# Keeping step 1's exponentials in an attention kernel, and who issues its block swaps

## The chip, the cores and the metric

The kernel runs on one core of a Trainium2 chip. A time is the device time of one execution in microseconds; the median of the runs is compared. TensorE (PE) multiplies matrices into PSUM, VectorE (DVE), ScalarE (ACT) and GpSimd (POOL) work element by element, and SyncE (SP) issues DMAs. GpSimd issues some of the DMAs too.

## The reference

`x` is 8 × 512 × 512 (batch, sequence, model). Sixteen heads of 32 columns attend within each batch, a condition token is projected and added to queries and keys, and the result is added to x:

```
Q, K, V = heads(x @ Wq.T + bq), heads(x @ Wk.T + bk), heads(x @ Wv.T + bv)
cQ, cK  = Q + heads(cond @ Wq.T + bq), K + heads(cond @ Wk.T + bk)
attn    = softmax(cQ @ cK.T / sqrt(32))          # 512 x 512 for each head
out     = x + merge(attn @ V)
```

## The kernel before

The work is cut into 32 steps, t = 0 to 31. Step t is a batch b = t // 4 and a group of four heads, r = t mod 4, which fill the 128 partitions (32 columns each). In what follows "tile t" is what belongs to step t.

For each tile the scores are first computed with queries on the partitions (`row_scores`, L641), in four blocks of 128 queries (`qc`), four heads each, one PSUM bank for a head. VectorE takes the negated row maxima from them (`row_max`, with single reductions of one bank at L589, or a reduction over a pair of neighbouring banks at L650). ScalarE takes the exponentials with that maximum as bias and adds up their sums (`denominators`, L693). These exponentials have the queries on the partitions, and the product with V needs the keys there. There are two ways on:

- An ordinary tile throws them away, keeping the sums. Its maxima are split into three bfloat16 parts (`split_max`, on GpSimd, L707 to L710) and transposed by a DMA (`turn_max`, L719). The scores are computed a second time with the keys on the partitions: four bursts (`exponentials`), each a small matmul that brings the maxima in (L745) and four matmuls for the scores (L748), then ScalarE's exponentials (L758).
- A kept tile (`KEPT`, steps 2 to 28) writes the exponentials of its first two query blocks to a place in SBUF (`room`). VectorE transposes them in blocks of 32 × 32 (`turn_kept`, L660, four instructions of 128 × 1024). What is left is to exchange the blocks between partitions. `swap_kept` does it by DMA for the six pairs of partition groups, in three rounds (`move`) of six transfers of 128 KB, L674: round 0 copies one block of each pair aside, round 1 copies the other over it, round 2 copies the first from aside. A round's transfer waits for the landing of its pair's transfer before. Rounds 0 and 1 are issued at the end of the step before, round 2 within the step. Only the other two query blocks are computed a second time, in two bursts (`exponentials_of_rest`, L766, L777, L787).

In step t, TensorE does the second scores of tile t, the row scores of tile t + 1 (and the first block of t + 2), the product with V of tile t − 1 (`weighted`, L792 for ordinary, L808 for kept tiles: first the half that was computed again, then the kept half) and one part of the projections of the next batch. These are computed by Strassen's scheme (`product`, L461) from sums of blocks of x (`combine_x`, L387 to L391, four sums for each batch) and of W. The list `MADE` spreads them over steps of a batch, three to a step. A kept step has three parts (`thirds`), an ordinary one four. After the products, ScalarE copies and GpSimd adds (`first_by_others`, L535 to L537 for q and k, L1220 and L1221 for v), or VectorE adds with the bias (`other_products`, L551 and L486). `send` transposes the result on VectorE (L880), scales it and adds x on GpSimd (L881, L882), and stores it through SP (L885). SP also loads x for the next batch (L173) and for the residual (L191).

The order on PE, DVE, ACT and POOL is that of the program text; the order of SP's DMAs is planned by the framework. Each queue is worked in order, so an instruction that waits holds up those behind it. The functions `begin` and `released` choose the PSUM banks of a part by the order in which they came free.

Steps with t mod 4 = 0 make the sums of x for the next batch on GpSimd, in parts 2 and 3, just before the rounds 0 and 1 of the next tile (t mod 4 = 1) are issued. Before the main loop, step 0 makes the first half of the sums for batch 1 on VectorE (L387, L388 at the end of its third part) and step 1 the second half on GpSimd.

Of the kernel before, what the change touches and what calls it, by code (L numbers as in the profile page):

```python
# [17 lines left out]
def kernel(  # L18
# [38 lines left out]
    nc = tc.nc  # L57
    P = 128
# [9 lines left out]
    T = B * G  # L68
    HS = S // 2

    KEPT = range(2, T - 3)
    KQ = NS // 2

    const = ctx.enter_context(tc.tile_pool(name="const", bufs=1))
# [54 lines left out]
    def advance():  # L129
        turn[0] += 1  # L130
# [67 lines left out]
    def bias_residual(t):  # L198

        if turned_by_vector(t):  # L200
            bias = bvs[:, t % G, :].unsqueeze(1).broadcast_to([P, NB, BL])
        else:
            bias = bvl.broadcast_to([P, S])
        nc.gpsimd.tensor_tensor(xr[t], xr[t], bias, ALU.add)  # L204
# [3 lines left out]

    def room(t):

        at = (t - KEPT[0]) % 3 * 4
        return store[:, at : at + 4].rearrange("p g c (h s) -> p g c h s", s=P)

    ring_at = [0]

    places = [*range(4, 16), *range(8, 12)]

    def chunk():

# [321 lines left out]
    def other_products(n, b, u, dens, small, at, bias=False):  # L541

        dens()
        one_, two_ = banks(at[0]), banks(at[1])
        product(n, b, u, 4, one_[:, :HS])
        product(n, b, u, 5, one_[:, HS:])
        small()
        product(n, b, u, 2, two_[:, :HS], (1,))
        product(n, b, u, 3, two_[:, HS:])
        c1, c12, c2, c22 = parts_of(n, b, u)  # L550
        nc.vector.tensor_tensor(c12, one_[:, HS:], c12, ALU.add)  # L551
        if bias and n != "v":
            plus(n, b, u, 1, c2, halves(one_), twice(c22))
        else:
            nc.vector.tensor_tensor(c2, halves(one_), twice(c22), ALU.add)
        plus(n, b, u, 0, c1, halves(two_), c1)
        if n != "v":
            for g in range(2):
                qkT[n, b * G + u * 2 + g] = pair_of(b * G + u * 2, n)[:, g, :]
# [104 lines left out]

    def swap_kept(t, move, last=nc.gpsimd):

        def part(a, g):
            return kept[t][a * BL : (a + 1) * BL, g].rearrange("p c h s -> p (c h s)")

        for n, (a, g) in enumerate(APART):  # L670
            at = (n + 2) % HG * BL
            aside = between[at : at + BL, n // HG].rearrange("p i s -> p (i s)")
            to, of = [(aside, part(a, g)), (part(a, g), part(g, a)), (part(g, a), aside)][move]
            (last if move == 2 or move == 0 and n >= 3 else nc.sync).dma_start(to, of)  # L674

    def denominators(t, qc, w=HG, js=range(HG)):

# [387 lines left out]
    row_max(1, 2)  # L1065
    denominators(1, 2)
    other_products("v", 0, 0, nothing, nothing, (0, 2))
    advance()
    exponentials(0, 2)
    row_max(1, 3)  # L1070
    split_max(1)
    turn_max(1)
    first_products("v", 0, 1, lambda: denominators(1, 3), nothing, 1)
    combine_x(1, 0)
    advance()
    exponentials(0, 3)
    row_max(2, 0)
    other_products("v", 0, 1, lambda: denominators(2, 0), nothing, (0, 2))

    MADE = [  # L1080
        (n, u, product)
# [26 lines left out]
        else:  # L1108
            released(1, 2, 4, 5, 6, 7, 0, 3)

    def bursts(s, i):

        if s not in KEPT:
            return [(s, i)]
        return [(s, i - 2)] if i >= 2 else []

    TURNED = {(0, 2): 2, (1, 2): 1, (2, 2): 1}
    TURNED_FIRST = {(0, 2): 1, (1, 2): 1, (2, 2): 1, (3, 2): 1}
    turned = {}

    def turn_more(t, i, after):

        behind = t - 1 not in KEPT
        for _ in range((TURNED if t in KEPT else TURNED_FIRST).get((i, after), 0)):
            if t + 1 in KEPT:
                n = turned[t + 1] = turned.get(t + 1, -1) + 1
                turn_kept(t + 1, n)
        if (t, i, after) == (1, 1, 1) or t in KEPT and (i, after) == (0, 2):
            turn_x((t - 1) % G + ((t - 1) // G + 2) * NC)

    def thirds(t, made):

        b, r = divmod(t, G)
        of = (t - 1) // G + 1
        begin(0, HG)
        turn_more(t, 0, 0)
        row_max_aside(t + 1, 1)
        max_aside(t + 1, 1)
        row_max(t + 1, 2, False, HG)
        turn_more(t, 0, 1)  # L1140
        denominators(t + 1, 1, None, (1, 2, 3, 0))
        denominators(t + 1, 2, HG)
        weighted(t - 1, banks(0), banks(1), nothing)
        turn_more(t, 0, 2)
        load_blocks()
        one_item(of, *next(made), (2, 3), ignore, nothing)
        released(0, 1, 4, 5, 6, 7, 2, 3)
        for i in (1, 2):
            begin(HG)
            exponentials_of_rest(t, i - 1)  # L1150
            turn_more(t, i, 0)
            rows = (t + 1, 3) if i == 1 else (t + 2, 0)
            row_max(*rows, False, HG)
            turn_more(t, i, 1)
            if i == 1:
                if t + 1 in KEPT:
                    swap_kept(t, 2)
                split_max(t + 1)
                if t + 1 in KEPT:
                    turn_max(t + 1)  # L1160
                else:
                    swap_kept(t, 2)
            dens = lambda js=range(HG): denominators(*rows, HG, js)
            n, u, kind = next(made)
            if kind == "first":
                products(of, n, u, kind, False, dens, nothing, None)
                turn_more(t, i, 2)
            elif n == "v":
                small = nothing
                if t + 1 not in KEPT:  # L1170
                    small = lambda: transpose_max(t + 1, banks(2), nc.scalar.copy)
                other_shared(of, n, u, dens, (0, 3), small, lambda: turn_more(t, i, 2))
                released(1, 2, 4, 5, 6, 7, 0, 3)
            else:
                products(of, n, u, kind, False, dens, nothing, False)
                turn_more(t, i, 2)
            if i == 1:
                aparts[t] = masked(t)
            load_blocks()
            if i == 2:  # L1180
                if r == 0:
                    combine_x(b + 1, 1, nc.gpsimd)
                load_residual(t + 1)
                if t + 1 in KEPT:
                    for move in range(2):
                        swap_kept(t + 1, move)
            else:
                bias_residual(t)
                if r == 0:
                    combine_x(b + 1, 0, nc.gpsimd)  # L1190

# [42 lines left out]
        else:  # L1234
            other_products(n, b, u, dens, nothing, at, True)

    for t in range(1, T - 3):
        b, r = divmod(t, G)
        made = iter(MADE[(t - 1) % G * 3 :])
        if t in KEPT:  # L1240
            thirds(t, made)
            continue
        items = "PVPP" if t - 1 in KEPT else "VPPP"
        for i, item in enumerate(items):
            rows = (t + 1, i + 1) if i < 3 else (t + 2, 0)
            scores = bursts(t, i)
            alone = not scores
            w = 0 if alone else HG
            begin(w)
            for u, kc in scores:  # L1250
                if u in KEPT:
                    exponentials_of_rest(u, kc)
                else:
                    exponentials(u, kc)
            turn_more(t, i, 0)
            row_max(*rows, False, w)
            turn_more(t, i, 1)
            if i == 2:
                split_max(t + 1)
                turn_max(t + 1)  # L1260
            dens = lambda js=range(HG): denominators(*rows, w, js)

            def last():
                if i == 0 and r == 1:
                    combine_x(b + 1, 1, nc.gpsimd)
                if i == 1 and r == 0:
                    combine_x(b + 1, 0, nc.gpsimd)

            if item == "P":
                products((t - 1) // G + 1, *next(made), alone, dens, last, None if (t, i) == (1, 3) else True)  # L1270
            else:
                dens()
                last()
                if alone:
                    weighted(t - 1, banks(4), banks(5), nothing)
                    released(6, 7, 0, 1, 2, 3, 5, 4)
                else:
                    weighted(t - 1, banks(0), banks(1), nothing)
                    released(2, 3, 1, 4, 5, 6, 7, 0)
            turn_more(t, i, 2)  # L1280
            if i == 2:
                aparts[t] = masked(t)
                if t > 1:
                    bias_residual(t)
            load_blocks()
            if i == 3:
                load_residual(t + 1)
            if i == 3:
                for move in range(2):
                    swap_kept(t + 1, move)  # L1290
    row_of[0] = None
    places[:] = 6, 7, 16, 17, 12, 13, 14, 15, 8, 9, 10, 11
    ring_at[0] = 0
# [218 lines left out]
```

## Time and profile before

| | us |
|---|---|
| median of 3 runs (666.71 to 668.23) | 666.72 |
| the profiled execution | 667.76 |
| its span | 666.0 |
| PE busy | 652.7 |
| DVE busy | 589.9 |
| ACT busy | 542.0 |
| POOL busy | 423.6 |

The profile is one execution with every instruction's start and duration. "Busy" is the time in which an engine worked on something; the span is the time from the first instruction to the end of the last, and the execution's time has a little more around it. A wait row names who waited, for whom, the total, how often and the longest. A timeline row gives start, duration, engine, line, operation, what is written and read, how many instructions are merged, and in brackets how long the engine was idle ahead of it and what ended that.

### The profile page before, as it was taken

What the parts mean: (1) busy time and instruction counts of PE and PEld (TensorE: products, weight loads), DVE (VectorE), ACT (ScalarE), POOL (GpSimd) and SP (SyncE); (2) the same over time, 40 slices, a digit from 0 to 9 for tenths busy, and PEclk for the clock granted to TensorE, in tenths of its full rate; (3) what the DMA queues carried; (4) which work ended last, traced back from release to release, by engine and by line L of the source; (5) the groups of instructions that cost most, each with busy time, mean ns of one, the idle gap of its engine ahead of it and who ended that gap; (6) DMA issues with size and microseconds to landing.
All of it is one profiled execution on the core that took longest, in us unless ns stands there. A gap on an engine that the chain in (4) does not pass through costs nothing.

```text
span 666.0 us, 24768 instructions
## 1 busy us (share of the span) xinstructions
PE 652.7 (98%) x9812; PEld 349.4 (52%) x9812; DVE 589.9 (89%) x821; ACT 542.0 (81%) x1378; POOL 423.6 (64%) x668
## 2 busy tenths in 40 slices
PE   9999999999999999999999999999999999999993
PEld 7345445555555555555555555555555555555421
DVE  3698899999999999998999999999999989995793
ACT  2479988889888888988888898888889888887771
POOL 3541345787666876659757696667875597576531
PEclk9999999999999999999999999999999999999998
DMA  6633157778777787877897787779877757786111
GB/s 178 105 51 63 31 122 161 163 165 187 173 152 174 161 190 154 189 156 167 171 190 167 169 191 172 160 150 170 196 165 176 169 133 175 149 181 138 18 18 32
DMA packets 246183, 97.14 MB, mean 146 GB/s; under 512 B 228842, under 2 KB 229354, under 8 KB 246068
## 3 DMA queue, kind: packets, MB, share of 16 engines
q1 hardware_dynamic: 232644, 62.65, 49.3%
q0 software_dynamic: 11664, 31.87, 17.3%
q8 instruction: 77, 1.26, 0.9%
q10 hardware_dynamic: 1760, 1.05, 0.5%
q14 instruction: 38, 0.31, 0.1%
HBM read 19.75 MB, written 8.39 MB: 42 GB/s over the span
## 4 chain that ended last, share of the span: by engine, by line
PE 95%; DMA 2%; SPq 1%; DVE 1%; issue 0%; DVEq 0%
PE psum L461 43%; PE psum L641 19%; PE psum L808 15%; PE psum L777 7%; PE psum L792 3%; PE psum L766 3%; PE psum L748 2%; SPq L270 1%; PE psum L404 1%; DMA w_q<-in_L_cond_Wq_dram 1%; PE psum L745 1%; PE psum L1336 1%; PE psum L818 1%; DMA store<-in_x_dram 1%; DMA w_k<-in_L_cond_Wk_dram 0%; PE psum L843 0%
## 5 line engine op out<-in xcount | busy, mean ns | idle before, releaser
L693 ACT ACTIVATE psum<-psum,nmax 128x512 f32<-128x512 f32 x263 | 174.8, 670 | 5.0 <-DVE nmax L589 3.9
L589 DVE TENSOR_REDUCE nmax<-psum 128x1 f32<-128x512 f32 x219 | 140.5, 678 | 22.2 <-PE psum L641 19.6
L693 ACT ACTIVATE store<-psum,nmax 128x512 f32<-128x512 f32 x190 | 130.3, 700 | 33.3 <-DVE nmax L589 23.8
L650 DVE TENSOR_REDUCE nmax<-psum 128x2 f32<-128x1024 f32 x127 | 153.7, 1211 | 1.3 <-PE psum L641 1.3
L674 POOL DMA_DIRECT2D store<-store x243 | 121.7, 504 | 48.1 <-DMA store<-store 36.2
L641 PE MATMUL psum<-kT,qT 32*128 32x512 f32 x1024 | 146.7, 616 | 0.0
L787 ACT ACTIVATE store<-psum 128x512 f32<-128x512 f32 x216 | 111.5, 603 | 22.6 <-PE psum L777 22.6
L660 DVE STREAM_TRANSPOSE store<-store 128x1024 f32<-128x1024 f32 x108 | 129.5, 1217 | 0.0
L808 PE MATMUL psum<-store,v 128*32 128x256 f32 x1728 | 99.3, 381 | 0.0
L808 PEld LDWEIGHTS psum<-store,v 128*32 128x32 f32 x1728 | 53.2, 110 | 54.1 <-ACT wT_q L628 19.7
L641 PEld LDWEIGHTS psum<-kT,qT 32*128 32x128 f32 x1024 | 57.8, 183 | 37.3 <-issue 20.2
L881 POOL TENSOR_TENSOR res<-res,recs 128x512 f32<-128x512 f32 x30 | 31.4, 1047 | 69.0 <-DVE res L880 68.9
L693 ACT ACTIVATION_READ_ACCUMULATOR psum<-psum,nmax 128x1 f32 x263 | 56.3, 214 | 0.0
L777 PE MATMUL psum<-qT,kT 32*128 32x256 f32 x864 | 55.8, 373 | 0.0
L461 PE MATMUL psum<-wc_v,xc 128*32 128x256 f32 x768 | 47.7, 379 | 0.0
L204 POOL TENSOR_TENSOR xr<-xr,bvs 128x512 f32<-128x512 f32 x30 | 38.4, 1279 | 12.2 <-DMA x<-in_x_dram 11.4
L461 PE MATMUL psum<-xc,wc_k 128*32 128x256 f32 x720 | 44.5, 379 | 0.0
L461 PE MATMUL psum<-xc,wc_q 128*32 128x256 f32 x720 | 44.5, 379 | 0.0
L777 PEld LDWEIGHTS psum<-qT,kT 32*128 32x128 f32 x864 | 42.3, 184 | 3.4
L693 ACT ACTIVATION_READ_ACCUMULATOR store<-psum,nmax 128x1 f32 x190 | 40.8, 215 | 0.0
L882 POOL TENSOR_TENSOR res<-res,xr 128x512 f32<-128x512 f32 x30 | 38.4, 1279 | 2.4
L758 ACT ACTIVATE store<-psum 128x512 f32<-128x512 f32 x56 | 28.9, 603 | 9.3 <-PE psum L748 7.2
(198 smaller groups left out, 1046.3 us busy)
## 6 DMA issues: line engine op xcount, KB each, us to landing
store<-store SPq DMA_DIRECT2D x243, 128.0 KB, 2.8
store<-store POOLq DMA_DIRECT2D x243, 128.0 KB, 3.7
out_dram<-res SPq DMA_DIRECT2D x122, 64.0 KB, 3.6
xr<-in_x_dram SPq DMA_DIRECT2D x120, 64.0 KB, 3.4
x<-in_x_dram SPq DMA_DIRECT2D x112, 64.0 KB, 3.0
w_q<-in_L_cond_Wq_dram SPq DMA_DIRECT2D x4, 256.0 KB, 5.3
w_v<-in_L_cond_Wv_dram SPq DMA_DIRECT2D x16, 64.0 KB, 2.5
w_k<-in_L_cond_Wk_dram SPq DMA_DIRECT2D x16, 48.0 KB, 3.0
```

The lines of the kernel that those rows point to most:

```text
L204: nc.gpsimd.tensor_tensor(xr[t], xr[t], bias, ALU.add)
L461: nc.tensor.matmul(pt[r], still[:, r], moving, start=(kc == kcs[0]), stop=(kc == kcs[-1]))
L589: nc.vector.tensor_reduce(nmax[t][:, qc, j : j + 1, 0], pt, AX.X, ALU.max, negate=True)
L641: nc.tensor.matmul(pt, qkT["q", t][r, qc * P : (qc + 1) * P], qkT["k", t][r, :], start=True, stop=True,)
L650: nc.vector.tensor_reduce(nmax[t][:, qc, pr * 2 : pr * 2 + 2, 0], pt, AX.X, ALU.max, negate=True)
L660: nc.vector.transpose(e, e)
L674: (last if move == 2 or move == 0 and n >= 3 else nc.sync).dma_start(to, of)
L693: nc.scalar.activation(to, of, AF.Exp, bias=nmax[t][:, qc, j, :], accum_out=sums[t][:, qc, j, :],)
L777: nc.tensor.matmul(bank[j][:, i * HS : (i + 1) * HS], qkT["k", t][r, kc * P : (kc + 1) * P], qkT["q", t][r, rest], start=False, stop=(i == 1),
L787: nc.scalar.activation(e[:, i, :], bank[pr * 2 + i], AF.Exp)
L808: nc.tensor.matmul(pt[j * HD : (j + 1) * HD, half * HS : (half + 1) * HS], vs[b % 2][:, kc, (g * HG + j) * HD : (g * HG + j + 1) * HD], e, ...
L882: nc.gpsimd.tensor_tensor(y, y, xr.pop(t), ALU.add)
```

## The change

Step 1 becomes a kept step, so `KEPT` begins at 1 and the separate form of an ordinary step in the main loop goes. Its tile gets the place in SBUF that the rule of three places gives it, and the ring of places for the exponentials of step 0 changes so that they don't overlap. Its four transpositions and rounds 0 and 1 of its swaps are in step 0, and round 2 is in step 1 as in any kept step. Step 0's last row maxima of tile 1 are taken in four single reductions instead of two and a pair. All four sums of x for batch 1 are made by GpSimd in step 0. Finally, round 0 of every tile is shared out differently: before, SP issued three of its six transfers and GpSimd three. Now SP issues all six for tiles with t mod 4 = 1, and one of six for the others. Round 1 stays with SP, round 2 with GpSimd.

```
-    KEPT = range(2, T - 3)
+    KEPT = range(1, T - 3)
...
-        at = (t - KEPT[0]) % 3 * 4
+        at = (t + 1) % 3 * 4
...
-    places = [*range(4, 16), *range(8, 12)]
+    places = [*range(4, 8), *range(12, 16)]
...
     def swap_kept(t, move, last=nc.gpsimd):
+        later = 6 if t % 4 == 1 else 1
...
-            (last if move == 2 or move == 0 and n >= 3 else nc.sync).dma_start(to, of)
+            (last if move == 2 or move == 0 and n >= later else nc.sync).dma_start(to, of)
...
     other_products("v", 0, 0, nothing, nothing, (0, 2))
+    turn_kept(1, 0)
     advance()
     exponentials(0, 2)
-    row_max(1, 3)
+    row_max(1, 3, True)()
     split_max(1)
     turn_max(1)
     first_products("v", 0, 1, lambda: denominators(1, 3), nothing, 1)
-    combine_x(1, 0)
+    turn_kept(1, 1)
+    turn_kept(1, 2)
+    combine_x(1, 0, nc.gpsimd)
     advance()
     exponentials(0, 3)
     row_max(2, 0)
     other_products("v", 0, 1, lambda: denominators(2, 0), nothing, (0, 2))
+    turn_kept(1, 3)
+    combine_x(1, 1, nc.gpsimd)
+    aparts[0] = masked(0)
+    for move in range(2):
+        swap_kept(1, move)
...
-        for _ in range((TURNED if t in KEPT else TURNED_FIRST).get((i, after), 0)):
+        for _ in range(TURNED.get((i, after), 0)):
...
-        if (t, i, after) == (1, 1, 1) or t in KEPT and (i, after) == (0, 2):
+        if (i, after) == (0, 2):
             turn_x((t - 1) % G + ((t - 1) // G + 2) * NC)
...
-                bias_residual(t)
+                if t > 1:
+                    bias_residual(t)
...
-    for t in range(1, T - 3):
-        b, r = divmod(t, G)
-        made = iter(MADE[(t - 1) % G * 3 :])
-        if t in KEPT:
-            thirds(t, made)
-            continue
-        items = "PVPP" if t - 1 in KEPT else "VPPP"
-        for i, item in enumerate(items):
...
-                    swap_kept(t + 1, move)
+    for t in KEPT:
+        thirds(t, iter(MADE[(t - 1) % G * 3 :]))
```

More of the change, by code (lines that the diff above doesn't have):

```diff
@@ L1109, in products @@
             released(1, 2, 4, 5, 6, 7, 0, 3)
[L1111 to L1115, printed above, removed]
     TURNED = {(0, 2): 2, (1, 2): 1, (2, 2): 1}
-    TURNED_FIRST = {(0, 2): 1, (1, 2): 1, (2, 2): 1, (3, 2): 1}
     turned = {}
     def turn_more(t, i, after):
-        behind = t - 1 not in KEPT
-        for _ in range((TURNED if t in KEPT else TURNED_FIRST).get((i, after), 0)):
+        for _ in range(TURNED.get((i, after), 0)):
             if t + 1 in KEPT:
@@ L1235, in one_item @@
             other_products(n, b, u, dens, nothing, at, True)
-    for t in range(1, T - 3):
-        b, r = divmod(t, G)
-        made = iter(MADE[(t - 1) % G * 3 :])
-        if t in KEPT:
-            thirds(t, made)
-            continue
-        items = "PVPP" if t - 1 in KEPT else "VPPP"
-        for i, item in enumerate(items):
[L1245 to L1289, printed above, removed]
-                    swap_kept(t + 1, move)
+    for t in KEPT:
+        thirds(t, iter(MADE[(t - 1) % G * 3 :]))
     row_of[0] = None
```

## The prediction

> **What bounds the kernel now.** I read the busy times and the chain of waits on the page first, then busy time by step, the waits, and the timelines of the two places that the change touches.
>
> ```profile
> PE 652.7 (98%) x9812; PEld 349.4 (52%) x9812; DVE 589.9 (89%) x821; ACT 542.0 (81%) x1378; POOL 423.6 (64%) x668
> PE 95%; DMA 2%; SPq 1%; DVE 1%; issue 0%; DVEq 0%
> ```
>
> TensorE is busy 98% of the span and is 95% of the chain that ended last. Time is won only by taking work off TensorE or by closing a stall in its queue. A stretch by steps shows where such a stall is: steps 1, 2 and 3 from TensorE's first instruction of one to that of the next, then steps 9, 13, 17, 21 and 25, cut at the ScalarE copy of L628 (one in each step from 2 on).
>
> ```profile
> 67.59:89.27 21.68, 21.68 (x292) 10.13 (x288) 18.50 (x25) 19.40 (x50) 5.93 (x11) 1.00 0.27 45
> 89.27:108.83 19.56, 19.56 (x285) 9.66 (x281) 18.20 (x24) 17.15 (x47) 12.85 (x22) 1.00 0.74 160
> 108.83:127.99 19.16, 19.16 (x316) 10.57 (x312) 18.33 (x25) 16.47 (x43) 12.59 (x21) 1.00 0.74 163
> 225.62:244.79 19.17, 19.17 (x316) 10.69 (x315) 18.27 (x25) 16.67 (x44) 16.58 (x26) 1.00 0.80 174
> 302.71:322.30 19.59, 19.59 (x316) 10.96 (x315) 18.32 (x25) 16.75 (x43) 16.38 (x25) 1.00 0.79 170
> 380.22:399.86 19.64, 19.64 (x316) 10.77 (x315) 18.41 (x26) 16.84 (x44) 18.06 (x27) 1.00 0.81 176
> 457.78:477.60 19.82, 19.82 (x316) 10.95 (x314) 18.34 (x25) 16.86 (x43) 18.24 (x27) 1.00 0.92 176
> 535.53:555.28 19.75, 19.75 (x316) 10.97 (x315) 17.75 (x24) 16.86 (x44) 18.18 (x27) 1.00 0.74 164
> ```
>
> The columns are the stretch, its length, then busy time of PE, PEld, DVE, ACT and POOL, the granted clock, DMA share and GB/s. Step 1, which computes all its scores twice, takes 21.68 us; step 3 makes the same kinds of products (q first, q other, k first) in the kept form and takes 19.16. Steps 9 to 25 are one kind of step (t mod 4 = 1), and the last four are 0.42, 0.47, 0.65 and 0.58 us longer than step 9: 2.12 us together, with POOL busy up to 18.2 us of 19.8. The clock is 1.00 in all, so it explains nothing. Two rows of the waits and a timeline of step 13 say how GpSimd reaches TensorE.
>
> ```profile
> POOL res L881 <- DVE res L880: 68.9, 24, 5.0
> DVE qT L486 <- POOL qT L537: 1.1, 4, 0.3
> 309.29 1.52 POOL L674 DMA_DIRECT2D store<-store  x3
> 314.70 0.73 POOL L537 TENSOR_TENSOR qT<-qT 128x256 f32<-128x256 f32 x1
> 315.46 1.41 DVE L486 SCALAR_TENSOR_TENSOR qT<-psum,tok,qT 128x512 f32<-128x512 f32 x2 [0.27 <-POOL qT L537]
> 239.46 1.08 PE L641 MATMUL psum<-kT,qT 32*128 32x512 f32 x8
> 316.54 1.51 PE L641 MATMUL psum<-kT,qT 32*128 32x512 f32 x8
> ```
>
> In step 13 VectorE's bias addition L486 waits for GpSimd's L537, and TensorE's row scores L641, which need the bank that L486 empties, take 1.51 us against 1.08 at the same place in step 9. The wait L486 <- L537 occurs exactly 4 times. GpSimd is late there because the sums of x (L387 to L391) and three swap issues of 1.52 us stand ahead of its work.
>
> **The change, part by part.**
>
> *Step 1 in the kept form.* Half of its second computation of the scores goes: four bursts become two.
>
> ```profile
> 73.28 0.39 PE L745 MATMUL psum<-maxT,onesb 3*128 3x512 bf16 x4
> 74.36 1.02 PE L641 MATMUL psum<-kT,qT 32*128 32x512 f32 x8
> 97.51 0.39 PE L766 MATMUL psum<-maxT,onesb 3*128 3x512 bf16 x4
> 98.60 1.21 PE L641 MATMUL psum<-kT,qT 32*128 32x512 f32 x8
> ```
>
> A full burst runs from 73.28 to 74.36, 1.08 us; step 1 has four. A burst of the rest runs from 97.51 to 98.60, 1.09 us; a kept step has two. That is 2.14 us off TensorE; the other 0.38 of the 2.52 between 21.68 and 19.16 are pauses between four parts that become three. ScalarE loses eight exponentials too, but it is off the chain. I take −2.52 us, if step 1 starts in step with its VectorE work. Bounds: 2.14 (the matmuls alone) and 2.52.
>
> *What step 0 pays.* VectorE gets four transpositions and one reduction in two singles, and sheds two sums of x.
>
> ```profile
> L660 DVE STREAM_TRANSPOSE store<-store 128x1024 f32<-128x1024 f32 x108 | 129.5, 1217 | 0.0
> 59.17 1.29 DVE L589 TENSOR_REDUCE nmax<-psum 128x1 f32<-128x512 f32 x2 [1.26 <-PE psum L641]
> 60.38 1.21 DVE L650 TENSOR_REDUCE nmax<-psum 128x2 f32<-128x1024 f32 x1
> 62.71 0.68 DVE L387 TENSOR_TENSOR xc<-xT 128x512 f32<-128x512 f32 x1
> 63.42 0.69 DVE L388 TENSOR_TENSOR xc<-xc,xT 128x512 f32<-128x512 f32 x1
> 64.37 1.29 DVE L589 TENSOR_REDUCE nmax<-psum 128x1 f32<-128x512 f32 x2 [0.26 <-PE psum L641]
> 67.79 0.69 DVE L483 TENSOR_TENSOR v<-psum,v 128x512 f32<-128x512 f32 x1
> 108.83 2.08 PE L641 MATMUL psum<-kT,qT 32*128 32x512 f32 x16
> 110.80 0.65 DVE L589 TENSOR_REDUCE nmax<-psum 128x1 f32<-128x512 f32 x1
> 119.66 1.29 DVE L589 TENSOR_REDUCE nmax<-psum 128x1 f32<-128x512 f32 x2 [0.59 <-PE psum L641]
> ```
>
> 4 × 1.217 + 0.08 (two singles of 1.29 for a pair of 1.21) − 0.68 − 0.69 = 3.58 us more. The first transposition falls into the idle 1.26 us before 59.17: hidden. The next two take 2.34 us where the sums took 1.40 up to 64.11 with 0.26 idle behind, so the reduction at 64.37 starts about 0.74 later. The last one follows L483, which then ends at 69.2 instead of 68.48, so VectorE's first maximum of step 1 starts at 70.3. In step 3 that maximum starts 1.97 us after TensorE's first row scores (110.80 − 108.83); in step 1 it would be due at 67.59 + 1.97 = 69.56. VectorE enters step 1 0.74 us late. TensorE itself needs no result of VectorE for its first instructions there; the lag reaches it later, through ScalarE, whose exponentials and copies wait for the maxima and empty the banks. The idle 0.59 us of such a step (row at 119.66) takes most of the lag up. I take +0.35 us, between 0 and 3.58 (no idle time usable).
>
> *Sums of x on GpSimd and 18 more swaps.* The two sums that VectorE sheds come on GpSimd just ahead of the two that it makes already.
>
> ```profile
> 66.48 1.29 POOL L390 TENSOR_TENSOR xc<-xT 128x512 f32<-128x512 f32 x1 [3.60 <-PE psum L461]
> ```
>
> They take 2 × 1.29 = 2.58 us of its 3.60 idle, and their first reader is a product of step 1. SP issues 12 swaps for tile 1, then has the stores of tile 0 and x behind them; GpSimd issues 6 within step 1, with the split of the next maxima and its copy to maxT behind them. The DMA share in step 1 is 0.27, so all this has room: 0 us. If that cover fails, tile 1's product in step 2 waits, at worst by a transfer.
>
> *Another share of issues.* Tiles with t mod 4 = 1 move three first-round issues from GpSimd to SP, the others move two from SP to GpSimd.
>
> ```profile
> L674 SPq DMA_DIRECT2D store<-store x243: 507/541/2282, 91.4 to 604.7; - x122
> L674 POOL DMA_DIRECT2D store<-store x243: 489/489/677, 92.4 to 609.5; - x122
> 307.64 8.24 SPq L674 DMA_DIRECT2D store<-store  x9
> 320.58 0.49 POOL L674 DMA_DIRECT2D store<-store  x1 [2.56 <-DMA store<-store]
> DMA to landing us min/median/max: 2.8/2.8/2.8
> 323.15 3.66 PE L808 MATMUL psum<-store,v 128*32 128x256 f32 x64
> ```
>
> For the six tiles 5 to 25, GpSimd is free 1.52 us earlier just ahead of L881 and L535 to L537. The largest excess of a step is 0.65 us, so all 2.12 us come back: −2.12 (bounds: 0, if something else stands behind it, and 2.12). For the other 21 tiles GpSimd gets 2 × 0.49 = 0.98 us more ahead of L881, which waits 68.9 / 24 = 2.87 us for VectorE on average: hidden, 0 us. Their swaps get shorter on SP (7 issues for 9), so GpSimd's third round and the split of the maxima behind it come no later.
>
> The price could be the transfers of tiles with t mod 4 = 1. SP now takes 8.24 us for 9 issues of 0.54, the rest is waiting for landings. With 12, the six of the first round last 6 × 0.6 = 3.6 us, by when the first has landed, and the six of the second follow: 7.2 us. So the chain ends about where it did. In step 13 the last transfer, issued at 320.58, lands 2.8 us later at 323.38 (the landing row is that one transfer's); the second half of L808's matmuls, which alone read the kept part, begins at 323.15 + 1.83 = 324.98. Slack 1.6 us.
>
> One thing could speak against more issues on GpSimd. VectorE transposes 1.217 us at a time and is busy 89% of the span, and yet the 243 issues on GpSimd take 489 ns in the median and 677 at most. By this row an issue is never held. [...]
>
> **Sum.** −2.52 + 0.35 − 2.12 = −4.29 us. The profiled execution took 667.76 us, with a span of 666.0 and 1.76 around it: 663.47. It lies 1.04 above the median of the three runs shown, 666.72, for which the sum gives 662.4.
>
> **Rivals.**
>
> *VectorE's new work in step 0 isn't hidden.* All 3.58 us reach TensorE: 666.72 − 2.52 + 3.58 − 2.12 = 665.7. For it: VectorE is 18.3 of 19.2 us busy in a step, so a lag is worked off slowly. Against it: the idle 1.26 us before 59.17.
>
> *The share of issues gives nothing (it doesn't do what it says).* What GpSimd no longer issues, it waits for in the next round, or the 2.12 us have another source: 666.72 − 2.17 = 664.55. For it: GpSimd waited 2.56 us for a landing at 320.58. Against: L881 starts in step 13 without a wait, and its lateness is what the 1.52 us cure.
>
> *Slower: the swaps of tiles 5 to 25 land late.* If three more issues on SP each cost more than their issue time, the third round is issued and lands later and L808 waits in the next step. With 1.6 us of slack a delay costs (d − 1.6) in each of six steps; the gain of 4.29 is used up at d = 2.3. If each of the three waits for a landing of 1.0 us beyond its turn, d = 3.0: 662.4 + 6 × 1.4 = 670.8. For it: the longest SP issue takes 2.28 us, and DMA share is 0.8 to 0.9 in these steps. Against: the sum of 7.2 us above.
>
> *Slower: GpSimd's issues are held by VectorE's transpositions.* Two more per tile at 0.489 + 1.217 make 3.41 us against the cover of 2.87: 0.54 late, at 21 tiles 11 to 12 us, 674. The maximum of 677 ns speaks against it. [...]
>
> **How the numbers follow.** Forecast 0.70, VectorE not hidden 0.07, no gain from the share 0.12, late swaps 0.07, held issues 0.02, something not seen 0.02. What a measurement can tell from no change is 0.3%, 2 us, so faster means under 664.7. The forecast and half of the 664.55 case lie there, and half of the unseen: 0.77. The other half and the VectorE case make 0.14 for the same, the rest 0.09 slower. The forecast's own range is 661.0 to 664: no lag at all and step 2 also down from 19.56 to 19.16 would give 661.7, less 0.7 for runs that stall less. The full range goes up to 665.8, which takes in the first two rivals and leaves out the slower ones.
>
> **What would show it.** Right: step 1 19.2 to 19.6 us long; steps 13, 17, 21 and 25 at 19.2; no wait L486 <- L537; L881 in those steps waiting for VectorE again. Wrong: L808 idle in the middle of a group behind a swap; SP over 10 us for its 12 issues; step 0 longer, or VectorE without idle time all through steps 1 and 2.

## The result and the profile after

The change brings the median from 666.71 us (five runs, 665.47 to 668.23) to 657.23 us (five runs, 656.78 to 658.96). The ratio is 0.987, with a 95% interval of 0.9854 to 0.9886. The forecast was 662.4 with a range from 661.0: the sign was right, and the gain of 9.5 us is more than twice the 4.3 expected.

The profiled execution of the kernel after took 658.96 us, with a span of 657.0. From its page, the busy times and the shares of the chain that ended last; then a table of busy time by step, with the columns of the prediction's table. The first stretch is step 1, from TensorE's first instruction of it to that of step 2, as in the prediction; the others are cut at the ScalarE copy of L628 and are steps 13, 15, 16, 17, 21 and 25.

```profile
PE 649.0 (99%) x9836; PEld 349.7 (53%) x9836; DVE 591.8 (90%) x823; ACT 539.4 (82%) x1372; POOL 442.8 (67%) x702
PE 92%; DMA 3%; SPq 2%; DVE 1%; issue 1%; ACT 0%; POOL 0%; DVEq 0%; ACTq 0%; POOLq 0%
```

```profile
67.21:86.77 19.56, 19.56 (x284) 9.76 (x280) 18.88 (x26) 17.12 (x45) 10.35 (x19) 1.00 0.77 157
300.08:319.25 19.17, 19.17 (x316) 10.70 (x314) 18.27 (x25) 16.68 (x44) 15.37 (x21) 1.00 0.84 179
338.63:359.33 20.70, 19.39 (x313) 10.96 (x309) 18.11 (x24) 16.89 (x44) 14.88 (x25) 1.00 0.89 175
359.33:379.06 19.73, 19.73 (x316) 10.74 (x318) 18.62 (x27) 16.93 (x45) 15.84 (x26) 1.00 0.78 167
379.06:398.23 19.17, 19.17 (x316) 10.70 (x315) 18.27 (x25) 16.69 (x44) 14.18 (x22) 1.00 0.81 174
456.16:475.34 19.18, 19.18 (x316) 10.71 (x315) 18.27 (x25) 16.68 (x44) 14.03 (x22) 1.00 0.80 170
533.27:552.44 19.17, 19.17 (x316) 10.57 (x315) 17.68 (x24) 16.68 (x44) 13.30 (x21) 1.00 0.65 148
```

Step 1 takes 19.56 us, 2.12 less than the 21.68 of before, where −2.17 was forecast. Steps 13, 17, 21 and 25 take 19.17 or 19.18 each, 2.11 us less together than the 78.80 of before. Steps 15 and 16 take 1.88 us more than a pair beside them (19.17 and 19.38). Step 2 loses 0.17 us (19.55 to 19.38). Step 1 also began 0.38 us earlier (67.21 against 67.59), which says nothing of the change: in the other executions with the ordinary step 1 it begins anywhere from 66.1 to 68.2. Together that is −2.9 us up to the last computation. The span lost 9.0. The rest lies behind the last work, at a place that the prediction did not look at. From the kernel before: the last row of the chain in order of time; then, at the last line of the kernel, the closing instructions of GpSimd's queue, and the last issues on ScalarE's queue (count: shortest/median/longest ns, first and last start).

```profile
655.89 0.61 DVEq L1507
```

```profile
L1507 POOLq EVENT_SEMAPHORE  x4: 17/17/17, 665.2 to 665.9; - x4
L1507 POOLq DRAIN  x3: 34/102/11361, 653.8 to 665.7; - x3
L1437 ACTq DMA_DIRECT2D out_dram<-res x2: 379/430/480, 655.2 to 656.7; - x2
SPq L1507 <- PEq L1507: 6.5, 2, 6.0
```

The same rows of the kernel after:

```profile
653.06 0.61 DVEq L1458
```

```profile
L1458 POOLq EVENT_SEMAPHORE  x4: 17/17/17, 656.3 to 656.9; - x4
L1458 POOLq DRAIN  x3: 34/102/3927, 651.0 to 656.8; - x3
L1388 ACTq DMA_DIRECT2D out_dram<-res x2: 380/430/480, 652.4 to 653.8; - x2
SPq L1458 <- PEq L1458: 0.7, 2, 0.5
```

In the kernel before the chain's last row ends at 656.50, and the span at 666.0. The last DMA is issued by 657.2 (656.7 + 0.48), but GpSimd's first closing DRAIN starts at 653.8 and lasts 11.36 us, to 665.2, where its first closing semaphore follows. SP waits 6.0 us of that time in one piece, among the closing semaphores (the row puts it down to PE's queue, whose own first closing semaphore stands at 665.4, behind GpSimd's at 665.2). In the kernel after, the DRAIN lasts 3.93 us, to 654.9, and SP's last landings come later: 2.3 us after an issue at 653.8, with SP's first closing DRAIN at 656.2 and GpSimd's first closing semaphore at 656.3 behind them. So the last issue came 2.9 us earlier, and what stands behind it, up to the end of the span, got 6.1 us shorter (8.8 to 2.7): 9.0 together.

Where most of the 1.88 us of steps 15 and 16 comes from, by the landing of the last five transfers that GpSimd issued for tile 14 (its third round), between 334.8 and 336.8, and TensorE's timeline:

```profile
DMA to landing us min/median/max: 5.0/5.4/5.5
```

```profile
342.73 1.93 PE L810 MATMUL psum<-store,v 128*32 128x256 f32 x32 [1.31 <-issue]
```

The last one, issued at 336.8, lands 5.4 us later, and the product L810 stands still for 1.31 us before its kept half. That is the prediction's "swaps land late", but on tile 14, one of those that moved issues to GpSimd, and in this execution: in step1_only below steps 15 and 16 cost 0.36 us over such a pair (19.18 and 19.73), and its span of 655.0 is within 0.1 us that of three of the five runs of the kernel after. That the new share made tile 14 late is not shown.

### The profile page after: what moved, and what is told of

It is laid out like the page before. It is cut to its first block, busy times and chain, and to the rows that moved or that the text cites. A ratio compares the mean times of both kernels' runs of the same rounds, so it can differ in the third digit from the quotient of the medians.

```text
span 657.0 us, 24808 instructions
## 1 busy us (share of the span) xinstructions
PE 649.0 (99%) x9836; PEld 349.7 (53%) x9836; DVE 591.8 (90%) x823; ACT 539.4 (82%) x1372; POOL 442.8 (67%) x702
## 4 chain that ended last, share of the span: by engine, by line
PE 92%; DMA 3%; SPq 2%; DVE 1%; issue 1%; ACT 0%; POOL 0%; DVEq 0%; ACTq 0%; POOLq 0%
PE psum L461 42%; PE psum L641 18%; PE psum L810 15%; PE psum L779 7%; PE psum L768 3%; PE psum L794 2%; DMA store<-store 2%; SPq L270 1%; PE psum L750 1%; PE psum L404 1%; DMA store<-in_L_cond_Wk_dram 1%; PE psum L1287 1%; PE psum L820 1%; PE psum L747 0%; DVE nmax L650 0%
## 5 line engine op out<-in xcount | busy, mean ns | idle before, releaser
L695 ACT ACTIVATE psum<-psum,nmax 128x512 f32<-128x512 f32 x255 | 169.4, 669 | 4.8 <-DVE nmax L589 3.9
L676 POOL DMA_DIRECT2D store<-store x273 | 136.1, 503 | 42.0 <-DMA store<-store 27.1
L695 ACT ACTIVATE store<-psum,nmax 128x512 f32<-128x512 f32 x197 | 135.3, 701 | 34.7 <-DVE nmax L589 25.3
L789 ACT ACTIVATE store<-psum 128x512 f32<-128x512 f32 x224 | 115.7, 602 | 23.4 <-PE psum L779 23.4
L660 DVE STREAM_TRANSPOSE store<-store 128x1024 f32<-128x1024 f32 x112 | 134.2, 1218 | 0.0
L810 PE MATMUL psum<-store,v 128*32 128x256 f32 x1792 | 103.1, 381 | 1.3 <-issue 1.3
L810 PEld LDWEIGHTS psum<-store,v 128*32 128x32 f32 x1792 | 55.2, 110 | 57.5 <-ACT wT_q L628 20.5
L883 POOL TENSOR_TENSOR res<-res,recs 128x512 f32<-128x512 f32 x30 | 31.4, 1047 | 60.2 <-DVE res L882 60.0
L779 PE MATMUL psum<-qT,kT 32*128 32x256 f32 x896 | 57.9, 373 | 0.0
L695 ACT ACTIVATION_READ_ACCUMULATOR psum<-psum,nmax 128x1 f32 x255 | 54.2, 213 | 0.0
L461 PE MATMUL psum<-xT,wT_k 128*32 128x256 f32 x480 | 34.5, 382 | 0.0
```

Of the source, the lines that this page charges most:

```text
L461: nc.tensor.matmul(pt[r], still[:, r], moving, start=(kc == kcs[0]), stop=(kc == kcs[-1]))
L660: nc.vector.transpose(e, e)
L676: (last if move == 2 or move == 0 and n >= later else nc.sync).dma_start(to, of)
L695: nc.scalar.activation(to, of, AF.Exp, bias=nmax[t][:, qc, j, :], accum_out=sums[t][:, qc, j, :],)
L779: nc.tensor.matmul(bank[j][:, i * HS : (i + 1) * HS], qkT["k", t][r, kc * P : (kc + 1) * P], qkT["q", t][r, rest], start=False, stop=(i == 1),
L789: nc.scalar.activation(e[:, i, :], bank[pr * 2 + i], AF.Exp)
```

## The experiments

Two theories were there from the result on: the closing DRAIN depends on how many transfers GpSimd issued (A), or the kept step 1 or the order of work makes it short (B); that it varies from execution to execution by itself (C) had to be excluded. The share of issues sets the count, so the first four runs vary it.

**share_only: the share of issues without the kept step 1** (267 issues on GpSimd).

```
# kernel before
+        later = 6 if t % 4 == 1 else 1
-            (last if move == 2 or move == 0 and n >= 3 else nc.sync).dma_start(to, of)
+            (last if move == 2 or move == 0 and n >= later else nc.sync).dma_start(to, of)
```

> The kernel before with the new share of the first-round issues alone; step 1 stays an ordinary step. GpSimd issues 6 x 6 + 21 x 11 = 267 transfers (243 before, 273 in the changed kernel). For the steps all theories expect the same: the wait L486 <- L537 gone, steps 13, 17, 21 and 25 at 19.2 us, 2.1 us less up to the last computation. They differ on GpSimd's last drain, which took 11.36 us in the profile of before and 3.93 in that of the changed kernel. Theory A (the drain depends on how many transfers GpSimd has issued): not 11.36 but some other length, so 658 to 660 us if it is short. Theory B (a kept step 1 shortens it): 11.4 us again and 664.5. Theory C (it is a chance of the execution): either, and different between executions of one kernel.

Measured: 660.8 us (kernel before beside it: 664.9), ratio 0.9937, interval 0.9901 to 0.9972. GpSimd's DRAIN, and two steps where the swaps or GpSimd are late again (steps 17 and 21):

```profile
L1509 POOLq DRAIN  x3: 34/102/3439, 653.7 to 660.2; - x3
```

```profile
380.42:400.37 19.95, 19.39 (x316) 11.04 (x315) 18.42 (x26) 16.84 (x43) 14.97 (x18) 1.00 0.78 163
458.32:478.02 19.70, 19.70 (x316) 11.40 (x314) 18.30 (x25) 16.75 (x43) 17.49 (x26) 1.00 0.90 182
```

The DRAIN is short with step 1 as it was, so B falls as the only cause. The four steps were expected at 19.2 us each and two of them were not, so the time stayed above the 658 to 660 us expected. In step 21 L486 waits for L537 again (0.3 us, once), although none of GpSimd's first-round issues stand ahead of it any more.

**step1_only: the kept step 1 with the share as it was** (252 issues).

```
# kernel after
-            (last if move == 2 or move == 0 and n >= later else nc.sync).dma_start(to, of)
+            (last if move == 2 or move == 0 and n >= 3 else nc.sync).dma_start(to, of)
```

> The changed kernel with the old share (three first-round issues on SP, three on GpSimd), so step 1 is kept and GpSimd issues 28 x 9 = 252 transfers. Steps: step 1 about 19.5 us long, 2.2 to 2.5 us won; the wait L486 <- L537 and the longer steps 13 to 25 are back. Drain: theory A some length of its own; theory B 3.9 us, so about 658.4 us in all; theory C either. If neither part alone shortens the drain, 664.3 us.

Measured: 656.8 us, ratio 0.9878, interval 0.9845 to 0.9912. That is the whole gain, without the other share; the nine issues of tile 1 alone bring the count from 243 to 252.

```profile
L1458 POOLq DRAIN  x3: 34/102/2214, 648.5 to 654.5; - x3
```

```profile
299.10:318.27 19.17, 19.17 (x316) 10.71 (x315) 18.27 (x25) 16.67 (x43) 17.43 (x26) 1.00 0.82 178
453.67:472.84 19.17, 19.17 (x316) 10.70 (x315) 18.26 (x25) 16.67 (x43) 15.08 (x24) 1.00 0.79 173
```

Steps 13 and 21 (and 17 and 25) are 19.17 us long although the three issues still stand ahead of GpSimd's work there. The 2.12 us are not bound to the share.

**round0_sp and round0_pool: the count alone, far to both sides** (162 and 324 issues).

```
# kernel before, round0_sp
+            (last if move == 2 else nc.sync).dma_start(to, of)
# kernel before, round0_pool
+            (last if move == 2 or move == 0 else nc.sync).dma_start(to, of)
```

> The kernel before with all of round 0 on SP: GpSimd issues 27 x 6 = 162 transfers. Steps 13 to 25 at 19.2 us, since GpSimd has 1.5 us less there. Drain: theory A a length that fits neither 11.36 nor 3.93 by need; if it grows with the number, well under 11; theory B 11.4 us; theory C either.

> The kernel before with all of round 0 on GpSimd: it issues 27 x 12 = 324 transfers. Steps 13 to 25 longer than before, by about the 1.5 us that GpSimd gets in addition in each of the six steps, if nothing else gives way: up to 9 us. Drain: theory A a third length; if it grows with the number, over 11 us, if it shrinks with it, under 3.9; theory B 11.4 us; theory C either.

Measured: 662.81 and 662.38 us, one run each. What was expected of the steps did not come: in round0_sp step 21 takes 20.57 us (and step 24 20.73), and in round0_pool only step 13 of the four is long (19.96), 77.48 us together against 78.80 before. The DRAINs:

```profile
L1507 POOLq DRAIN  x3: 34/102/4737, 654.4 to 660.4; - x3
```

```profile
L1507 POOLq DRAIN  x3: 34/102/8087, 651.7 to 660.3; - x3
```

Sorted by the number of issues, the DRAIN lasted 4.74, 11.36, 2.21, 3.44, 3.93 and 8.09 us at 162, 243, 252, 267, 273 and 324. It does not grow with the count throughout, as theory A had it first. But from 162 to 243 it grows by 6.62 us over 81 issues, 0.082 us each; from 252 to 324 by 5.88 over 72, 0.082 each; between 243 and 252 it falls by 9.2. That made theory D: a sawtooth of the count.

**before_252 and after_243: nine issues across the fall, in both directions.**

```
# kernel before, before_252
+            (last if move == 2 or move == 0 and n >= (2 if t % 3 == 0 else 3) else nc.sync).dma_start(to, of)
# kernel after, after_243
+            (last if move == 2 or move == 0 and n >= (4 if t % 3 == 0 else 3) else nc.sync).dma_start(to, of)
```

> The kernel before with one first-round issue more on GpSimd in the nine tiles divisible by 3 (n >= 2), so that GpSimd issues 252 large transfers. Theory D: drain 2.2 us and the time 5.8 us less than before, give or take 0.5 for what the moved issues do in the steps. Theory B and C: the time of before, within 1 us.

> The kernel after with the issues of step1_only (n >= 3), but in the nine tiles divisible by 3 one more first-round issue goes to SP (n >= 4), so that GpSimd issues 243 instead of 252. Theory D: the closing DRAIN comes back to 11.36 us; it starts about 5.8 us before the end as in step1_only and now ends the span, so the time is 5.7 us more than step1_only's 656.8, about 662.5, although the steps take what they take there. Theory B: the drain stays at 2 to 4 us and the time within 0.5 us of 656.8.

Measured: before_252 took 660.35 us against 666.28 of the kernel before beside it, ratio 0.9907 (0.9886 to 0.9928); after_243 took 663.97 us, ratio 0.9966 (0.9935 to 0.9997). Nine issues moved in the one kernel win 5.9 us; nine moved in the other take back 5.9 us (0.9966 − 0.9878 is 0.88% of 666). DRAIN of before_252:

```profile
L1507 POOLq DRAIN  x3: 34/102/2207, 651.9 to 658.0; - x3
```

Of after_243, with SP's wait at the end:

```profile
L1458 POOLq DRAIN  x3: 34/102/11356, 650.2 to 662.1; - x3
SPq L1458 <- PEq L1458: 6.6, 2, 6.2
```

With 243 issues the DRAIN of the kernel with the kept step 1 is that of the kernel before to 5 ns. B and C are out. And after_243 has the DRAIN of before, the kept step 1 and nearly the old share: its 2.3 us below before (0.34%, between 0.03 and 0.65%) are what the change is worth without the end of the span. The shorter steps 1 and 2 make 2.3 us as well (2.12 and 0.17).

**before_small9 and before_small4: more issues that move next to nothing** (252 and 247).

```
# kernel before, n = 9 or 4, in the setup
+    extra = const.tile([P, n + 1, 2], F32, tag="extra", name="extra")
+    nc.vector.memset(extra, 0.0)
+    for i in range(n):
+        nc.gpsimd.dma_start(extra[:BL, i + 1, :], extra[BL : 2 * BL, 0, :])
```

> The kernel before with nine small transfers more on GpSimd (32 partitions of 8 bytes, inside SBUF, issued in the first microseconds), so that GpSimd issues 252 instead of 243; nothing else changes. The closing DRAIN of GpSimd lasted 4.73, 11.36, 2.22, 3.44, 3.92 and 8.09 us with 162, 243, 252, 267, 273 and 324 transfers: 0.082 us for each within 162 to 243 and 0.081 within 252 to 324, with a fall between 243 and 252. Theory D (the drain depends on the number of transfers that GpSimd has issued, as a sawtooth): the drain falls from 11.36 to about 2.2 us, SP's last landing ends the span, and the time falls by 5.8 us against the kernel before of the same job. Theory B (the drain is short where step 1 is kept) and theory C (chance): no change, the drain stays near 11.4. If bytes and not transfers count: no change.

> The kernel before with four small transfers more on GpSimd (247). It narrows where the sawtooth falls. Theory D: the drain is either 11.7 us (the fall lies above 247) with the time of before, or 1.8 us with a time 5.8 us less; no value between. Theories B and C: 11.4 us or a random value.

Measured: 676.57 us (ratio 1.0152, 1.0107 to 1.0197) and 673.82 us (one run). The DRAIN did what D said:

```profile
L1511 POOLq DRAIN  x3: 34/102/2207, 668.5 to 675.3; - x3
```

```profile
L1511 POOLq DRAIN  x3: 34/102/11681, 659.6 to 671.8; - x3
```

Transfers of 256 bytes count like those of 128 KB, 247 is still on the rising side (11.68), and the fall lies between 247 and 252. But the time went up by 10.3 and 7.5 us, in steps of up to 23 us: a miss that asked for its own cause, the addresses behind the new tile (E) or the small transfers (F).

**before_same_room9, before_extra_only, before_extra_128: count and address apart.**

```
# kernel before, before_same_room9
+    for i in range(9):
+        nc.gpsimd.dma_start(xc[:BL, i % 4, i // 4 % 2, i : i + 2], ones[BL : 2 * BL, :2])
# kernel before, before_extra_only (128: [P, 16, 2])
+    extra = const.tile([P, 10, 2], F32, tag="extra", name="extra")
+    nc.vector.memset(extra, 0.0)
```

> The kernel before with nine small transfers on GpSimd again, but between tiles that it has anyway (from ones to columns of xc, which are written over later), so that every address stays where it was. In before_small9 the drain was 2.21 us, as the count of 252 said, but steps 10 to 23 of the loop were up to 3.9 us longer. Theory E (the new tile shifted the addresses behind it by 80 bytes, and the large transfers got slower): here the steps are those of before, the drain is 2.2 us and the time 5.8 us less than before. Theory F (the small transfers themselves put the later ones of GpSimd's queue at worse places in its ring): the steps are as long as in before_small9, the time about 10 us more than before, drain 2.2.

> The kernel before with the new tile of before_small9 (80 bytes in each partition) and without any new transfer: GpSimd issues 243. Theory E: steps 10 to 23 as long as in before_small9, drain 11.36, so that the time is about 10 + 5.8 = 16 us more than before. Theory F: the time of before, within 1 us.

> before_extra_only with a tile of 128 bytes in each partition in place of 80, no new transfers. before_extra_only was 18.5 us slower than before, with steps of up to 23.9 us. Theory G (what matters is how the large tiles behind it are aligned, and 128 is a multiple of the 64 bytes and of the 32 that 80 is not): the time of before, within 1 us. Theory H (any shift of the tiles against each other or against the start is enough): 10 to 20 us more than before.

Measured: before_same_room9 660.17 us against 665.12, ratio 0.992 (0.9903 to 0.9938). before_extra_only 683.66 us, ratio 1.0262 (1.0203 to 1.0321). before_extra_128 665.35 us, ratio 1.0004 (0.9992 to 1.0016). The first one:

```profile
L1509 POOLq DRAIN  x3: 34/102/2207, 651.5 to 657.5; - x3
SPq L1509 <- PEq L1509: 0.7, 2, 0.5
```

Nine transfers that do nothing for the result, issued in the first 8 us, make the kernel before 5.0 us faster (5.8 were expected): the plainest proof of D. Two steps of before_extra_only, its waits over these steps, and its DMA queues (packets, MB, share of 16 engines' span):

```profile
302.24:324.74 22.50, 21.09 (x316) 11.70 (x315) 18.53 (x25) 16.98 (x44) 18.83 (x30) 1.00 0.73 150
324.74:348.50 23.76, 21.14 (x316) 11.34 (x314) 18.27 (x26) 17.13 (x45) 14.89 (x26) 0.93 0.91 168
```

```profile
POOL store L676 <- DMA store<-store: 10.3, 6, 4.8
PEld L768 <- DMA maxT<-split: 3.1, 1, 3.1
```

```profile
q0 software_dynamic: 11664, 31.87, 18.9%
```

The queues of before_extra_128:

```profile
q0 software_dynamic: 11664, 31.87, 18.1%
```

Eighty bytes in front of the large tiles, with no new transfer, cost 18.5 us, and 128 bytes cost nothing: F and H are out, and E stands. For G, that it is the alignment, speak the one shift of 128 bytes without a cost (0.1 us) and the shifts of 80 (18.5) and of 40 (the tile of before_small4, 7.5 with its four transfers) with one; other shifts were not run, and which multiple of bytes would count, of those that the expectation names or another, no run shows. The packets are the same 11664, 48 for each of the 243 issues; those of GpSimd's queue took 18.9% of 675.9 us in the one and 18.1% of 663.5 in the other, 6% longer. The kernel before, with the same time as the 128 bytes, has 17.3% of 666.0 us, 4% less than they, so the packets' time alone doesn't give the price. With the 80 bytes GpSimd waits up to 4.8 us for a landing in these steps, and the transfer of the maxima comes late for TensorE, which waits 3.1 us for it. Where the tiles start, and why the one shift costs time and the other none, no run here shows.

**after_280: one share for all tiles in the kernel after** (280 issues).

```
# kernel after
-            (last if move == 2 or move == 0 and n >= later else nc.sync).dma_start(to, of)
+            (last if move == 2 or move == 0 and n >= 2 else nc.sync).dma_start(to, of)
```

> The kernel after with one share of issues for all tiles (n >= 2), 280 on GpSimd. The drain by the count is 2.22 + 28 x 0.081 = 4.5 us and ends before SP's last landing. If the share by tiles (six more on SP where t mod 4 is 1) is worth the 2.12 us that the prediction gave it, steps 13, 17, 21 and 25 are 0.4 to 0.7 us longer here and the time is 659; if keeping step 1 had removed those waits already, as step1_only's steps of 19.17 us suggest, the time is that of after, 657.2, within 0.5 us.

Measured: 656.95 us, ratio 0.9873 (0.9857 to 0.989), with a DRAIN of 4.49 us, as the count said (4.5).

```profile
L1458 POOLq DRAIN  x3: 34/102/4492, 649.0 to 654.7; - x3
```

```profile
453.51:473.27 19.76, 19.76 (x316) 10.96 (x315) 18.35 (x25) 16.88 (x43) 18.20 (x27) 1.00 0.80 170
```

Only step 21 is long again (19.76); steps 13, 17 and 25 are 19.17. after, step1_only and after_280 are within 0.5 us of each other and none beats the others: the share is worth nothing that can be measured, apart from the count that it gives. Beside their own runs of the kernel before, step1_only and after_280 win 8.1 and 8.2 us, which is what the DRAIN (5.9) and the shorter steps 1 and 2 (2.3) make together. The 9.5 us of the result are 1.3 more, about half of what the executions of the kernel before differ by (665.47 to 668.23); what they are made of is open.

## Why the prediction was wrong, point by point

- **Step 1 in the kept form, −2.52, and step 0's lag, +0.35: right in size, the lag by another road.** Together −2.17 on 21.68 makes 19.51; the step takes 19.56 us, and 19.56 to 19.58 in step1_only, after_243 and after_280. The lag, 0.40 us over step 3's 19.16, stands at the very start of the step:

```profile
67.21 2.48 PE L641 MATMUL psum<-kT,qT 32*128 32x512 f32 x16
67.85 0.51 PEld L641 LDWEIGHTS psum<-kT,qT 32*128 32x128 f32 x2 [0.33 <-ACT store L695]
67.03 0.69 ACT L695 ACTIVATE store<-psum,nmax 128x512 f32<-128x512 f32 x1 [0.28 <-DVE nmax L650]
69.59 0.65 DVE L589 TENSOR_REDUCE nmax<-psum 128x1 f32<-128x512 f32 x1
```

  TensorE's first row scores take 2.48 us against 2.08 in step 3, because they wait for ScalarE, which waited for a maximum of VectorE in step 0. VectorE's first maximum comes 2.38 us after TensorE's start, 0.41 later than in step 3. The prediction had VectorE 0.74 us late (0.68 where its own rows are added up: 2.34 − 1.40 − 0.26), with TensorE touched only later and most of the lag taken up by idle time. That half of a larger lag and the whole of a smaller one are nearly the same number is luck.
- **Sums of x on GpSimd, 0: right**, nothing on TensorE in steps 0 to 2 waits for them.
- **The share of issues, −2.12: the number came, the reason did not.** The four steps fell from 78.80 to 76.69 us, and the wait of L486 for L537 has gone. But step1_only has 76.68 with the old share, before_same_room9 has 77.11 (with the old form too), share_only 77.99 and after_243 78.40. With the old share these steps take between nothing and 2.1 us too much. The rival "the share gives nothing, the 2.12 us have another source" was right in its condition. What shows of that source is in GpSimd's timeline of step1_only, ahead of step 13, which begins at 299.10 there:

```profile
295.67 0.49 POOL L676 DMA_DIRECT2D store<-store  x1 [1.02 <-DMA store<-store]
...
306.62 1.06 POOL L883 TENSOR_TENSOR res<-res,recs 128x512 f32<-128x512 f32 x1
```

  The last issue of the round ahead, which waits for a landing, stands 3.43 us before the step; in the kernel before it stood 2.84 before it (299.87 against 302.71). All of GpSimd's work behind it is as much earlier, and L883 begins 7.52 us into the step against 8.11 for the same work. In the kernel after it stands 2.28 before it (297.80 against 300.08). Why it differs, is not settled.
- **SP's 12 issues, 7.2 us: 9.17**, 2 us more than the sum gave. Still under the 10 that would have made it wrong, and tile 13 was not late.
- **The swaps of moved tiles: partly seen.** Not tiles 5 to 25 but tile 14 was late, in the profiled execution, for 1.5 us over step1_only.
- **GpSimd's issues held by VectorE: fell.** 273 issues, 492 ns in the median and 677 at most (243 in the kernel before: 489 and 677). No run shows an issue held for the 1.217 us of a transposition, the term that makes the 674 us of that rival: in none of them did a swap issue on GpSimd take longer than 677 ns.

```profile
L676 POOL DMA_DIRECT2D store<-store x273: 492/492/677, 79.6 to 606.7; - x137
304.93 9.17 SPq L676 DMA_DIRECT2D store<-store  x12
```

- **The sum, the step that failed.** "The profiled execution took 667.76 us, with a span of 666.0 and 1.76 around it": it took the 666.0 us as filled by the steps, so that every term came off the end and nothing else could. There was no term for what stands between the last work and the end of the span. That was 9.5 us from the end of the chain at 656.50, of which GpSimd's DRAIN of 11.36 us was the longest part. The share of issues was costed by issue time alone (1.52 us less on GpSimd for six tiles, 2 × 0.49 us more for the others); that the whole change also brings GpSimd's transfers from 243 to 273, and that their count has a price at the end, was not in the sum. The DRAIN runs from 3.3 us before the last issue, and SP's landings end 2.2 us after that issue, so about 5.5 us of it are covered; 11.36 − 5.5 gives 5.9 us that come back when the DRAIN is short, in addition to the 4.29.

With that term the forecast would have been 666.72 − 4.29 − 5.9 = 656.5. That this is near the measured 657.23 is in part luck, since it still has the −2.12 of the share, which the runs put at nothing. What they show is 5.9 + 2.12 + 0.17 = 8.2 us, or 658.5.

## What to carry to other kernels

Read the end of the span before summing: compare the end of the chain and the last issue with the end of the span, and list the closing instructions of each queue, since a gap there is time that no step explains. An edit that moves DMAs to or from GpSimd's queue should be judged by how many it issues in all, too: here 243 or 252 made 5 to 6 us, and nine transfers of 256 bytes were worth half of what the whole change brought. And an experiment that adds a tile should leave the others where they are: here a shift by 80 bytes cost three times what was to be measured, and only a shift by 128 was seen to cost nothing.

## What the runs showed of the hardware that was not expected

In these runs GpSimd's closing DRAIN lasts by the number of transfers that it has issued, the ones of 256 bytes like those of 128 KB, and although the last of them was issued 44 us before (609.5 against 653.8 in the kernel before):

| issues on GpSimd | DRAIN, us |
|---|---|
| 162 | 4.74 |
| 243 (before, after_243, two with an extra tile) | 11.36, 11.36, 11.36, 11.35 |
| 247 | 11.68 |
| 252 (step1_only, before_252, two with small transfers) | 2.21, 2.21, 2.21, 2.21 |
| 267 | 3.44 |
| 273 | 3.93 |
| 280 | 4.49 |
| 324 | 8.09 |

Between these counts it rises by 0.082 us with each and falls once, between 247 and 252, by 9.9 us (12.09 extended to 252, less 2.21), which is what 121 issues add. In the kernels before and after it begins with GpSimd's last addition (1.28 us from 653.88 in the one, 1.27 from 651.04 in the other), so about 1.3 us of its length lie under that. What GpSimd does in that time, where other falls lie, and whether the 0.082 us hold for transfers of other shapes than these, is open. The second surprise is what a shift does: 80 bytes more in front of the large tiles made 18.5 us, 128 bytes nothing. That the transfers got slower by it is what the landings above suggest; why is open.
